# A four-layer gated cross-attention and expert network on one core: context steps ahead, joined projections, and a reordered first stage

## The chip, the core and the metric

The kernel runs on one core of a Trainium2 chip. The metric is device time in microseconds (us). The kernel before was run three times: 908.18 median, 906.4 to 910.17. One more execution was profiled, and all views below come from it.

The engines that matter here: TensorE (PE) multiplies, and its weight loads (PEld) overlap its passes; VectorE (DVE), ScalarE (ACT) and GpSimd (POOL) do the elementwise work; SyncE (SP) issues most DMAs. Each works through its own queue in order.

## The reference

The state x has 16 sequences of 128 tokens with 128 features, and there is a context of the same shape. Eight steps follow each other, each on the layer-normalised x, each gated by a tanh and added:

```python
x = x + tanh(g_xattn[0]) * L0_xattn(ln(x), ctx)   # q + tril(c c^T) q, no softmax
x = x + tanh(g_ffn[0])   * L0_ffn(ln(x))          # 8 experts of 256, top 2
x = x + tanh(g_xattn[1]) * L1_xattn(ln(x), ctx)   # one head, projections in two steps
x = x + tanh(g_ffn[1])   * L1_ffn(ln(x))          # 16 experts of 128, grouped top 4, and shared ones
x = x + tanh(g_xattn[2]) * L2_xattn(ln(x), ctx)   # 16 heads of 8, masked
x = x + tanh(g_ffn[2])   * L2_ffn(ln(x))          # 64 slots, top 8, a gated recurrent update
x = x + tanh(g_xattn[3]) * L3_xattn(ln(x), ctx)   # 16 heads, half of them at half resolution
x = x + tanh(g_ffn[3])   * L3_ffn(ln(x))          # 32 experts of 64, grouped top 8, and shared ones
```

The attention of layer 1 projects twice, with nothing between:

```python
h = lin(x, hW, hb);  c = lin(ctx, cW, cb)
q = lin(h, qW, qb);  k = lin(c, kW, kb);  v = lin(c, vW, vb)
return lin(softmax(q k^T / sqrt(128)) v + q, oW, ob)
```

## The kernel before

**Tiles.** The 16 sequences are four groups of four (GB = 4); the state of a group is X[g], 128 partitions by 512 numbers, and stays in SBUF. CT[g] is the context of a group, transposed, made in the first stage. Everything is in 32-bit floats, and a product of 128x512 shows as two passes.

**The expert layers.** `experts` (L1084) is a stream that walks ORDER: layer 0 for group 0 alone, then layer 1 and layer 3 for four groups each. Each chunk of 128 hidden units is pg and pu (L450, L451), an activation sg on ScalarE (and L456 on VectorE), h = sg * pu on VectorE (L462), hw = h * cb with the routing weights of the chunk on GpSimd (L470) or on VectorE where `on_vector` says so (L468), and two chunks later the product acc (L1092). A chain written out by hand (`in_turn`) keeps the expert products in this order on TensorE. cb is a row of routing weights spread over partitions by a DMA.

**Layer 0 for groups 1 to 3.** Here tokens are sorted by expert. `choose_0` routes them, `places_0` (L904) computes where each goes and issues 24 sends (L940), which are indirect DMAs from GpSimd's queue, a few behind each chunk of group 0 (SEND, and four more at L1161), and the last ones behind the latest rs (L1169). `blocks_0` (L977) reads the sorted rows back as xb (L1006), transposes them (L1013), and works through 31 blocks. `return_0` (L1055) fetches the results during layer 1.

**Who follows whom.** The attention of a group is written into the program when the stream has passed that group: `until(0, g)` pulls the stream until layer 0 is done for group g, then `attention_1(g)` is emitted whole, and so on for `attention_2` and `attention_3` (L1225 to L1229, L1330 to L1339). A scheduler then orders each engine's instructions by when it expects their inputs; `behind_of` pins an instruction behind another on its engine.

**attention_1** (L555) normalises and transposes x, then runs hT, cfT, qT, kT as four products of 128x512 with a biased copy on ScalarE each (L286), v as four products of 128x128, and scores, softmax, output. **attention_2** (L592) and **attention_3** (L729) normalise, transpose, and project queries (qT) and keys (kTm, in two masked copies on VectorE, L296) and values (vp, L480), then loop over sequences. kTm has one buffer, and so has vp.

**The first stage** (`linear_attention`, L509; FIRST, L1187) does layer 0's attention: transpose the context, products of it with itself, the causal mask on VectorE (sm, L522), the normalised x as xn, and the product with sm. `normed` (L246) is the statistics on VectorE (L251, L253), rs by a power on GpSimd (L257), and then either VectorE's subtract and multiply (L268) or, with `on_act`, off on GpSimd (L262, L263) and ScalarE's scale and bias (L266). `blank` (L133) makes zeroed tiles on GpSimd.

Of the kernel before, what the change touches and what calls it, by code (L numbers as in the profile page):

```python
# [59 lines left out]
def flamingo(ctx, tc, x_in, ctx_in, mask_in, w1, w2, w3, wslot, wsmall, slots, cols_in, rows_in, consts_in,  # L60
# [72 lines left out]
    def blank(name, shape):  # L133
        t = const.tile(shape, F32, tag=name, name=name)
        nc.gpsimd.memset(t[:], 0.0)
        return t
# [109 lines left out]
    def normed(g, xn=None, on_act=False):  # L246
# [3 lines left out]
        for t in range(GB):  # L250
            nc.vector.bn_stats(st[:, t, :], x[:, t, :])  # L251
# [8 lines left out]
        if on_act:  # L260
            off = small.tile([P, GB], F32, tag="off", name="off")
            nc.gpsimd.tensor_tensor(off[:], mv[:, :, 0], rs[:], ALU.mult)  # L262
            nc.gpsimd.tensor_scalar(off[:], off[:], -1.0, None, ALU.mult)  # L263
# [245 lines left out]
    def linear_attention(g):  # L509
# [12 lines left out]
        nc.vector.tensor_tensor(sm[:], ps, bc(tri[:], 1, GB), ALU.mult)  # L522
        yield
        xn = normed(g, act.tile([P, GB, D], F32, tag="a1", name="xn0"), on_act=True)
# [29 lines left out]
    w = lambda W, i: W[:, i * D:(i + 1) * D]  # L554
    def attention_1(g):  # L555
        _, xnT = normed_T(g)
        add_row(g, ob1)
        hT = linear_T(w(W1, 0), xnT, "a0", bias=col("hb"))
        cfT = linear_T(w(W1, 1), CT[g], "a1", bias=col("cb"))
        qT = linear_T(w(W1, 2), hT, "qT", bias=col("qb"))  # L560
        kT = linear_T(w(W1, 3), cfT, "kTm", bias=col("kb"), bufs=1)
        pv = split(mm_tile())
        for t in range(GB):
            mm(pv[:, t, :], cfT[:, t * P:(t + 1) * P], w(W1, 4))
        v = act.tile([P, GB, D], F32, tag="a3", name="v1")
        nc.vector.tensor_tensor(v[:], pv, bc(row("vb"), 1, GB), ALU.add)
# [15 lines left out]
        add_gated(g, py, tgx[:, 1:2])  # L582

# [8 lines left out]
    def attention_2(g):  # L592
        _, xnT = normed_T(g)
        add_row(g, ob2)
        qT = act.tile([P, 2, GT], F32, tag="qT", name="qT2")
        kTm = act.tile([P, 2, 2, GT], F32, tag="kTm", name="kTm2", bufs=1)
        for s in range(2):
# [4 lines left out]
            keys_by_head(kTm[:, s], W2H[:, 2 + s, :], CT[g][:], "bk2", s)  # L602
        pv = mm_tile()
        for t in range(GB):
            mm(pv[:, t * P:(t + 1) * P], CT[g][:, t * P:(t + 1) * P], w(W2, 0))
        values(GB, 0, NH, pv[:], bvr)
# [39 lines left out]
        add_gated(g, py, tgx[:, 2:3])  # L646

# [81 lines left out]
    def attention_3(g):  # L729
        _, xnT = normed_T(g)  # L730
        add_row(g, ob3)
        even = CT[g][:, 0:GT:2]
        G2 = GT // 2
        qT = act.tile([P, 3 * G2], F32, tag="qT", name="qT3")
        qa, qb = qT[:, 0:GT], qT[:, GT:]
        kTm = act.tile([P, 2, 3 * G2], F32, tag="kTm", name="kTm3", bufs=1)
        ka, kb = kTm[:, :, 0:GT], kTm[:, :, GT:]
        p = mm_tile()
        mm(p[:], W3H[:, 0, :], xnT[:])
        nc.scalar.activation(qa, p[:], AF.Identity, bias=hcol["bq30"])  # L740
        p = mm_tile()
        mm(p[:, :G2], W3H[:, 1, :], xnT[:, 0:GT:2])
        nc.scalar.activation(qb, p[:, :G2], AF.Identity, bias=hcol["bq31"])
# [8 lines left out]
        values(2, 8, 8, pv[:, 4 * 64:6 * 64], bv3r[:, 4 * 64:])  # L752
        oa = act.tile([P, 2, P], F32, tag="oT", name="oa3")
# [91 lines left out]
        for u in range(2):  # L845
            nc.vector.scalar_tensor_tensor(xv[:, :, u, :], py[u], tgx[:, 3:4], xv[:, :, u, :], ALU.mult, ALU.add)

# [14 lines left out]

    def on_vector(layer, g, n):

        return (layer, g) == (0, BYE - 1) and n > 5 and n % 2 == 0 or (layer, g) == (1, 0) and n < 4
# [218 lines left out]
    def experts():  # L1084
# [23 lines left out]
        for at, (layer, g) in enumerate(ORDER):  # L1108
# [10 lines left out]
            if moving:  # L1119
                for n, k in SEND:  # L1120
                    steps.setdefault(n, []).extend([("m", sending, None)] * k)
                steps.setdefault(13, []).append(("m", "owners", None))
            elif at + 1 < len(ORDER):
# [35 lines left out]
            if moving:  # L1159
                side[0] = "m"  # L1160
                for _ in range(4):  # L1161
# [52 lines left out]

    sending, fetching = places_0(), return_0()
# [8 lines left out]

    until(0, 0)  # L1225
    ob1 = gated_row("ob", tgx[:, 1:2])
    attention_1(0)
    until(0, 1)
# [189 lines left out]
```

## Time and profile before

| what | us |
|---|---|
| median of three runs | 908.18 (906.4 to 910.17) |
| profiled execution, its own time | 908.96 |
| its span, first to last instruction | 907.3 |
| VectorE busy | 571.6 |
| GpSimd busy | 302.0 |
| ScalarE busy | 267.6 |
| one chunk hw on GpSimd / h on VectorE | 1.289 / 0.684 |
| one biased copy of a projection on ScalarE (L286) | 0.687 |
| one masked copy of keys on VectorE (L296, 128x512) | 0.737 |

The stages in the span: first stage and routing to about 34 us; layer 0's experts for group 0 to 90; a stretch to 109; the blocks to 160; layer 1's experts with attention_1 to about 290; attention_2, the slots, attention_3 and layer 3's experts to the end, the last group's experts alone from about 860.

A line of the timeline has start, duration, engine, line, operation, output and inputs, shapes and count, and in brackets how long the engine had stood idle and what ended that. A wait for several things is put down to the one that came last.

### The profile page before, as it was taken

Reading aid. Unit: us, or ns where it says so; the run is one execution under the profiler, and the core shown is the slowest. Engines: PE = TensorE matmul, PEld = TensorE weight load, DVE = VectorE, ACT = ScalarE, POOL = GpSimd, SP = SyncE. Lnnn points to the kernel's source line nnn. Section 1 sums busy time; section 2 is a strip of 40 time slices with the busy share of each in tenths; the row PEclk is TensorE's granted clock in tenths of the full one; section 3 lists DMA queues with packets and bytes.
Section 4 is the critical chain, followed back from the end, with each engine's and each line's share of the span. In section 5 each row is a group of like instructions: output and inputs, shape, how many; then the busy total and the mean of one; then the engine's idle time right before and its main releaser. Section 6 shows DMA issues by size and latency. Waiting matters only on the chain. (4 is left out here: it accounts for less than half of the span.)

```text
span 907.3 us, 16095 instructions
## 1 busy us (share of the span) xinstructions
PE 832.2 (92%) x6191; PEld 465.8 (51%) x6191; DVE 571.6 (63%) x1597; ACT 267.6 (29%) x485; POOL 302.0 (33%) x312
## 2 busy tenths in 40 slices
PE   5898699898999999998999989999999999999997
PEld 4653399344545454554455554555554554555443
DVE  4673344557888657468676667768665668667532
ACT  2522355231322232422322322332222232222321
POOL 4348521556452114113421114321124123313443
PEclk9899799999999999999999999999999999999999
DMA  9441222631221012001212113210002111211230
GB/s 299 134 117 42 61 71 74 220 125 40 85 71 36 13 49 59 24 22 39 71 34 59 38 48 107 80 39 25 25 13 75 46 36 50 81 49 52 92 110 30
DMA packets 55677, 62.12 MB, mean 68 GB/s; under 512 B 14312, under 2 KB 33512, under 8 KB 55472
## 3 DMA queue, kind: packets, MB, share of 16 engines
q1 hardware_dynamic: 53536, 57.67, 20.6%
q0 software_dynamic: 1536, 3.15, 1.2%
q8 instruction: 49, 0.80, 0.4%
q10 hardware_dynamic: 528, 0.26, 0.1%
q14 instruction: 28, 0.23, 0.1%
HBM read 53.97 MB, written 7.09 MB: 67 GB/s over the span
## 5 line engine op out<-in xcount | busy, mean ns | idle before, releaser
L470 POOL TENSOR_TENSOR hw<-h,cb 128x512 f32<-128x512 f32 x137 | 176.6, 1289 | 446.6 <-DVE h L462 371.9
L451 PE MATMUL pu<-xnTx,wall 128*128 128x512 f32 x288 | 153.9, 616 | 7.6 <-DVE sg L456 6.2
L450 PE MATMUL pg<-xnTx,wall 128*128 128x512 f32 x288 | 153.7, 616 | 1.8 <-ACT xnTx L243 1.4
L455 ACT ACTIVATE sg<-pg 128x512 f32<-128x512 f32 x123 | 73.5, 598 | 264.1 <-PE pg L450 251.1
L1092 PE MATMUL acc<-hw,wall 128*128 128x512 f32 x288 | 149.9, 604 | 1.5 <-POOL hw L470 1.5
L462 DVE TENSOR_TENSOR h<-sg,pu 128x512 f32<-128x512 f32 x145 | 99.2, 684 | 62.8 <-PE pu L451 45.5
L456 DVE SCALAR_TENSOR_TENSOR sg<-sg,pg 128x512 f32<-128x512 f32 x123 | 83.5, 679 | 38.9 <-ACT sg L455 38.4
L451 PEld LDWEIGHTS pu<-xnTx,wall 128*128 128x128 f32 x288 | 51.7, 192 | 68.8 <-issue 40.5
L1092 PEld LDWEIGHTS acc<-hw,wall 128*128 128x128 f32 x288 | 53.8, 194 | 61.5 <-issue 53.6
L490 DVE TENSOR_REDUCE mp<-mm 128x4 f32<-128x512 f32 (+1 forms) x112 | 65.8, 645 | 21.1 <-PE mm L617 19.9
L450 PEld LDWEIGHTS pg<-xnTx,wall 128*128 128x128 f32 x288 | 49.8, 193 | 40.8 <-issue 29.0
L504 DVE RECIPROCAL rcw<-po 128x128 f32<-128x128 f32 (+1 forms) x28 | 25.2, 900 | 52.9 <-PE po L499 41.9
L257 POOL TENSOR_TENSOR rs<-ve,neghalf 128x4 f32<-128x4 f32 x32 | 32.8, 1026 | 63.0 <-DVE ve L255 59.4
L496 PE MATMUL po<-pts,vp 128*32 128x128 f32 (+1 forms) x896 | 45.9, 273 | 6.8 <-ACT pts L639 5.9
L639 ACT ACTIVATE pts<-mm 128x512 f32<-128x512 f32 x64 | 33.8, 601 | 55.0 <-PE mm L633 54.6
L268 DVE TENSOR_SCALAR xn<-x,mv,rs 128x128 f32<-128x128 f32 x96 | 35.5, 426 | 21.5 <-POOL rs L257 21.2
L499 PE MATMUL po<-pts,own 128*32 128x128 f32 (+1 forms) x896 | 44.0, 265 | 0.0
L496 PEld LDWEIGHTS po<-pts,vp 128*32 128x32 f32 (+1 forms) x896 | 21.5, 108 | 29.8 <-ACT pts L639 14.6
L241 PE MATMUL tr<-ident,xn 128*128 128x128 f32 x100 | 22.9, 310 | 13.4 <-DVE xn L268 12.2
L251 DVE BATCH_NORM_STATS2 st<-x 128x6 f32<-128x128 f32 x128 | 29.4, 280 | 7.9 <-DMA x<-in_x 7.3
L458 ACT ACTIVATE sg<-pg 128x512 f32<-128x512 f32 x33 | 19.5, 595 | 48.7 <-PE pg L450 46.1
L617 PE MATMUL mm<-kTm,qT 32*128 32x256 f32 x256 | 30.6, 414 | 0.0
(345 smaller groups left out, 1236.1 us busy)
## 6 DMA issues: line engine op xcount, KB each, us to landing
cb<-combD SPq DMA_DIRECT2D x72, 256.0 KB
cb<-combD SPq DMA_DIRECT2D x128, 128.0 KB
wall<-in_gu SPq DMA_DIRECT2D x24, 256.0 KB
wall<-in_dn SPq DMA_DIRECT2D x12, 256.0 KB
xb<-xd SPq DMA_DIRECT2D x7, 256.0 KB
yd<-yb SPq DMA_DIRECT2D x7, 256.0 KB
xd<-vp SPq DMA_DIRECT2D x1, 1072.0 KB
x<-in_x SPq DMA_DIRECT2D x4, 256.0 KB
```

The lines of the kernel that those rows point to most:

```text
L268: nc.vector.tensor_scalar(xn[:, t, :], x[:, t, :], mv[:, t, 0:1], rs[:, t:t + 1], ALU.subtract, ALU.mult)
L450: in_turn(chain, nc.tensor.matmul(out=pg[:], lhsT=w[:, 0], rhs=xnT[:], start=True, stop=True))
L451: in_turn(chain, nc.tensor.matmul(out=pu[:], lhsT=w[:, 1], rhs=xnT[:], start=True, stop=True))
L455: nc.scalar.activation(sg[:], pg[:], AF.Tanh, scale=0.5)
L456: nc.vector.scalar_tensor_tensor(sg[:], sg[:], 1.0, pg[:], ALU.add, ALU.mult)
L462: ins = nc.vector.tensor_tensor(h[:], sg[:], pu[:], ALU.mult)
L470: latest["hw"] = nc.gpsimd.tensor_tensor(hw[:], h[:], cb[:], ALU.mult).ins
L490: nc.vector.tensor_reduce(mp[:, 0:n, 32 * i + 16:32 * i + 18], src, AX.X, ALU.max)
L496: in_turn(chain, nc.tensor.matmul(out=po[32 * jj:32 * jj + 32, 0, :], lhsT=vcols, rhs=pts, start=first, stop=last, skip_group_check=True))
L499: in_turn(chain, nc.tensor.matmul(out=po[32 * jj:32 * jj + 32, 1, :], lhsT=own[rows, r, :], rhs=pts, start=False, stop=last, skip_group_ch ...
L639: nc.scalar.activation(pts[:], split(ps[i]), AF.Exp, scale=scale8)
L1092: in_turn(chain, nc.tensor.matmul(out=acc[0][:], lhsT=w[:, 2], rhs=h[:], start=n == 0, stop=last))
```

## The change

1. *Joined projections.* A new step `joined_1` computes once, from the weights of layer 1, the products of the first and second projection, and the joined biases. `attention_1` then has one product for q, one for k, four small ones for v, and no hT or cfT.
2. *Context steps.* attention_1, 2 and 3 first emit what needs the context alone (k, v; kTm, vp), yield, and emit the rest when the stream has passed (`attend`). The context step of group 0 is emitted in the stream, three chunks after the joining; kT takes buffer a0, no longer kTm.
3. *First stage.* Groups 0 and 1 are normalised by VectorE; of groups 2 and 3 the first statistic is pinned behind the sm of the group before; the memsets of `blank` are pinned behind group 2's off.
4. *Sends.* The last chunk (n = 15) of group 0 multiplies its routing weight on VectorE; two sends, not four, follow the last chunk, so that seven, not five, come behind the latest rs.

```diff
     def blank(name, shape):
         t = const.tile(shape, F32, tag=name, name=name)
-        nc.gpsimd.memset(t[:], 0.0)
+        behind_of("first", nc.gpsimd.memset(t[:], 0.0))
...
-    def normed(g, xn=None, on_act=False):
+    def normed(g, xn=None, on_act=False, behind=None):
...
         for t in range(GB):
-            nc.vector.bn_stats(st[:, t, :], x[:, t, :])
+            ins = nc.vector.bn_stats(st[:, t, :], x[:, t, :])
+            if t == 0 and behind is not None:
+                behind_of(behind, ins)
...
-        xn = normed(g, act.tile([P, GB, D], F32, tag="a1", name="xn0"), on_act=True)
+        xn = normed(g, act.tile([P, GB, D], F32, tag="a1", name="xn0"), on_act=g > 1, behind=("sm", g - 1) if g > 1 else None)
+        if g == 2:
+            latest["first"] = latest["off"]
...
+    def joined_1():
+        pt = tr_tile()
+        for i in range(2):
+            nc.tensor.transpose(pt[:, i * D:(i + 1) * D], w(W1, i), ident[:])
+        firsts = work.tile([P, 4, P], F32, tag="pts", name="firsts", bufs=3)
+        nc.any.tensor_copy(firsts[:, 0:2, :], split(pt)[:, 0:2, :])
+        p = mm_tile()
+        for i, (one, two) in enumerate(((0, 2), (1, 3), (1, 4))):
+            mm(p[:, i * D:(i + 1) * D], firsts[:, one, :], w(W1, two))
+        at = 3 * D
+        mm(p[:, at:at + 1], w(W1, 2), col("hb"))
+        mm(p[:, at + 1:at + 2], w(W1, 3), col("cb"))
+        cbs = work.tile([P, P], F32, tag="rcw", name="cbs")
+        nc.vector.tensor_scalar(cbs[:], ones[:], col("cb"), None, ALU.mult)
+        pb = mm_tile()
+        mm(pb[:, 0:D], cbs[:], w(W1, 4))
+        nc.vector.tensor_copy(W1[:, 0:3 * D], p[:, 0:3 * D])
...
     def attention_1(g):
+        kT = linear_T(w(W1, 1), CT[g], "a0", bias=col("kb"))
+        pv = split(mm_tile())
+        for t in range(GB):
+            mm(pv[:, t, :], CT[g][:, t * P:(t + 1) * P], w(W1, 2))
+        v = act.tile([P, GB, D], F32, tag="a3", name="v1")
+        nc.vector.tensor_tensor(v[:], pv, bc(row("vb"), 1, GB), ALU.add)
+        yield
         _, xnT = normed_T(g)
         add_row(g, ob1)
-        hT = linear_T(w(W1, 0), xnT, "a0", bias=col("hb"))
-        cfT = linear_T(w(W1, 1), CT[g], "a1", bias=col("cb"))
-        qT = linear_T(w(W1, 2), hT, "qT", bias=col("qb"))
-        kT = linear_T(w(W1, 3), cfT, "kTm", bias=col("kb"), bufs=1)
...
+        qT = linear_T(w(W1, 0), xnT, "qT", bias=col("qb"))
...
-        return (layer, g) == (0, BYE - 1) and n > 5 and n % 2 == 0 or (layer, g) == (1, 0) and n < 4
+        return (layer, g) == (0, BYE - 1) and (n > 5 and n % 2 == 0 or n == 15) or (layer, g) == (1, 0) and n < 4
...
+                steps.setdefault(JOIN, []).append(("m", joining, None))
+                steps.setdefault(JOIN + 3, []).append(("m", context_1, None))
...
-                for _ in range(4):
+                for _ in range(2):
                     next(sending)
...
+    def attend(attention, g, *what):
+        steps = attention(g)
+        next(steps)
+        until(*what)
+        next(steps)
...
     for g in range(NG + 1):
         if g < NG:
-            until(1, g)
-            attention_2(g)
+            attend(attention_2, g, 1, g)
         if g > 0:
-            until("slots", g - 1)
-            attention_3(g - 1)
+            attend(attention_3, g - 1, "slots", g - 1)
```

JOIN is 9, a chunk number of group 0. In attention_2 and attention_3 the lines for kTm and vp move unchanged ahead of the first yield.

## Prediction, before the changed kernel was run

> **What bounds the kernel now.** I read part 1 of the page, then the busy times by stage, then the timeline of the stretches where TensorE stands still.
>
> ```profile
> PE 832.2 (92%) x6191; PEld 465.8 (51%) x6191; DVE 571.6 (63%) x1597; ACT 267.6 (29%) x485; POOL 302.0 (33%) x312
> ```
>
> TensorE is busy 832 of 907 us; nothing else comes near. The next view has, for each stretch, its length and then the busy time (and records) of TensorE, its weight loads, VectorE, ScalarE and GpSimd, the granted clock and DMA.
>
> ```profile
> 86.00:109.00 23.00, 13.94 (x43) 6.76 (x41) 6.20 (x19) 3.92 (x6) 15.22 (x16) 0.78 0.20 62
> 109.80:160.00 50.20, 49.48 (x436) 48.90 (x437) 21.46 (x68) 30.15 (x57) 9.15 (x16) 1.00 0.24 68
> 217.00:300.00 83.00, 75.38 (x301) 38.16 (x299) 68.81 (x205) 21.33 (x37) 38.14 (x37) 0.98 0.18 54
> 300.00:860.00 560.00, 528.98 (x4909) 286.93 (x4907) 378.01 (x971) 157.07 (x281) 142.61 (x122) 0.99 0.16 50
> ```
>
> From 109.8 to 160 (the expert blocks of layer 0) and again from 300 to 860 TensorE sets the pace: work taken off it is time. From 217 to 300 VectorE is busy 69 of 83 us too. From 86 to 109 TensorE is not the limit, and the timeline (start, duration, engine, line, in brackets the idle time before and who ended it) tells what is:
>
> ```profile
> 88.82 1.12 PE L1092 MATMUL acc<-hw,wall 128*128 128x512 f32 x2 [1.04 <-POOL hw L470]
> ...
> 95.63 1.05 POOL L257 TENSOR_TENSOR rs<-ve,neghalf 128x4 f32<-128x4 f32 x1
> ...
> 97.20 1.33 PE L241 MATMUL tr<-ident,xn 128*128 128x128 f32 x4 [5.92 <-DVE xn L268]
> ...
> 99.20 2.07 PE L108 MATMUL mm<-xnTm,w 128*128 128x512 f32 x2 [0.68 <-ACT xnTm L243]
> ...
> 103.28 0.96 POOL L940 DMA_INDIRECT xd<-xs,to  x1 [0.30 <-issue]
> ...
> 108.50 0.66 PE L1013 MATMUL tr<-ident,xb 128*128 128x128 f32 x4 [0.74 <-DMA xb<-xd]
> ```
>
> GpSimd issues 24 row sends (one per 1.28 us) between 61.6 and 104.2; the blocks start only when the last has landed and the rows come back, 4.3 us later.
>
> **The change, part by part.** [...]I sum on the span.
>
> *First stage.* Before, the masked products sm of groups 0 and 1 wait on VectorE behind the statistics of group 2, which wait for its DMA at 11.10, and ScalarE's xn waits at 10.72 for GpSimd's off, behind memsets. After, the built order has ScalarE copy both context transposes. But only the first of group 2's four statistics is set behind; the other three still stand ahead of the new xn. So: DMA 11.10, three statistics 0.66, xn of group 0 4 x 0.33 = 13.1, two more xn 0.65, sm 14.4; the eight products of group 0 (1.9) end near 16.9, where the add of x started at 19.30 before. Two xn, sm and the rest follow under that. Layer 0's routing, its comb rows and the first expert chunk come about 2 us earlier (between 0 and 3). The moved memsets (2.4 us) now stand ahead of group 1's second rs, whose result is not due before the transposes of group 0's comb: nothing.
>
> *Expert stage of group 0 (34 to 90).* Added for TensorE: the joining (two transposes 0.22, eight passes of 128x128 0.9, four one-column passes 0.4: 1.5 us), and kT and v of group 0 (0.86 + 0.90 = 1.76), out of the gap. W1 was issued at 53.45 and by the byte rate of that stretch is there near 57; the join's transposes come at 60: no wait. The join falls ahead of a TensorE bubble of 1.1 us (73.2 to 74.3, ScalarE waiting on GpSimd) and costs 0.4 or less; kT and v cost 1.76. VectorE gains 1.7 us of joining where it is busy 58%: nothing. So TensorE arrives at the last chunks where it was (-2 + 2). The last hw goes from GpSimd (ready 88.76) to VectorE (0.69 after h, 87.5): the last acc starts 87.6, not 88.8. The chain acc, yT, transposes, add, ve (4.6 us) ends at 92.2, not 93.45. With two sends fewer ahead, GpSimd is free then: rs at 92.3, not 95.6. Behind it stand three sends, the row add (1.28) and now four sends, not two: the last is issued by 103.8, not 104.24. GpSimd's queue, not the attention, starts the blocks: **-0.5 us**, of 3.3 that rs gains.
>
> *The gap.* xnT, q, scores: two projections fewer and kT, v gone. This shortens 97 to 108 by some 5 us, and all of it goes into the wait for the sends. [...]Row: after 5.92 us idle two passes of 128x512 took 2.07, where the warm pair takes 1.02. [...]Before, TensorE worked from 97 until 107.8 and entered the blocks warm (eight passes in 1.06). [...]I take **+1.7**, since the row at 99.20 shows the half pace after such an idle.
>
> *Blocks.* kT and v of group 1 now lie here, TensorE full: **+1.8**. The blocks end 3.0 later; the fetches behind them, which pace 160 to 187, follow.
>
> *attention_1 of group 1.* Between 190.0 and 199.0 TensorE ran pg, hT, cfT, qT, kT, v, scores and pu, partly at half pace. After: pg 1.3, q 1.7, pu 1.0, scores 0.9, to 194.9: **-4.1**. Of groups 2 and 3 each: context 1.76 earlier (+1.0 where it fills part of a 1.64 us wait at 219, +1.8 for group 3), and hT, cfT, kT, v gone from the attention, 3.5: **-2.5 and -1.7**.
>
> *attention_2 and attention_3.* No work goes; 3.6 us of VectorE (four kTm of 0.74, vp 0.68) and about 3 of TensorE stand ahead of the wait for the expert group, not after it. TensorE's waits that this queue makes are mp's: 1.64 at 296.75, 0.74 at the start of each of four attention_3. At most 1.6 + 4 x 0.74 = 4.6 goes. Where attention_2 follows attention_3 directly nothing moves but the order. The added wait: kTm has one buffer, so its write waits for the last scores of the attention before, and h, sg and the next statistics stand behind it on VectorE. Below, -4.6; above, four to seven times an uncovered 3.6. After attention_2 of group 0 a dozen TensorE passes of 0.86 stand before the next xn transposes, so it is mostly covered: **-2**.
>
> Sum: -0.5 + 1.7 + 1.8 - 4.1 - 2.5 - 1.7 - 2.0 = **-7.3**: span 900.0, and on the median of runs 908.2 - 7.3 = 900.9.
>
> **Rivals.**
> (a) *As summed*, 900.9. For it: full TensorE on both sides, 5.2 us of passes gone for good (six linears of 0.86). Chance 0.52.
> (b) *The saving turns into waits.* From 217 to 300 VectorE has 69 of 83 us, loses nothing, and each attention's softmax is its work; if groups 2 and 3 give nothing (-4.2 lost) and mp's waits only move (-2 lost): 908.2 - 1.1 = 907. The first stage's 2 us not coming would cost 1.5 more. Against it: TensorE still worked 75 of those 83 us. Chance 0.24.
> (c) *Slower:* the context operations block VectorE at the head of its queue, at the seven transitions from one attention to the next; each holds h back by up to 3.6 us, and TensorE's in-order queue with it. It decides from 1.0 us uncovered per transition (7.3 / 7), and at 2.0 gives 900.9 + 14 = 915. For it: kTm's single buffer, VectorE 67% busy from 300 to 860. Against: the passes that lie between. Chance 0.11.
> (d) *More:* all of mp's 4.6 goes, no cold start (-1.7), and attention chains that are 3 us shorter take 2 more off later waits: 900.9 - 2.6 - 1.7 - 2 = 894.6. Chance 0.13.
> That a part doesn't do what it says is in the first stage: three of four statistics are not set behind. It takes 1 to 2 us there, most of which the sends would have swallowed.
>
> **How the numbers follow.** Likeliest 900.9. Case (a) alone spans 897 to 905: the bounds of the first stage, the cold start and the waits, 2 us each. The range reaches over (d) nearly and into (b): 894.5 to 909; outside lie (c) and the rim of (d). A measurement of this kernel tells about 0.5% (4.5 us) from no change: faster is below 903.6. From (a) most (0.46 of 0.52), (d) all, (b) 0.05: 0.64. Same: the rest of (a), most of (b), a little of (c): 0.25. Slower: 0.11.
>
> **What would show it.** First stage: the first add of x near 17, the first expert matmul near 31.5. rs behind the last add near 92, the last send issued near 104, transposes of xb near 108, the first block passes at twice 1.06 per eight. The blocks end near 163; scores of group 1 near 196 to 198; the last expert stage, 47 us long, starts about 7 earlier and is as long as before. I am wrong if the sends end later than 104.5, if new waits of TensorE on kTm, vp or h show at the transitions, or if the xb wait shrinks by more than 1 us.

## The result and the profile after

Ten runs of each kernel on one chip: the changed kernel 913.75 us median (907.71 to 915.30), the kernel before 908.5 (906.40 to 913.12). The ratio is 1.0045, with a 95% interval of 1.0025 to 1.0065: about 4 us slower (5 by the medians), where 7.3 less were predicted. The profiled execution took 915.29 us, span 913.6; before it was 908.96 and 907.3.

Part 1 of the page of the changed kernel (busy time, share of the span, instructions):

```profile
PE 831.8 (91%) x6189; PEld 466.9 (51%) x6189; DVE 578.4 (63%) x1610; ACT 260.7 (29%) x470; POOL 299.1 (33%) x307
```

This is the first thing to see. Eight products of 128x512 are gone (hT and cfT of four groups, 0.86 each, 6.9 us) and the joining brought 1.5, so TensorE should be busy 5.4 us less. It is busy 831.8 us, where it was 832.2, and it stands idle 81.7 us, where it was 75.0. The clock is a part of this: 46.5 us of its busy time lie in windows at half clock, where it was 31.0. These are the sums of the view of stretches over all half-clock windows, of the changed kernel and then of the kernel before:

```profile
sum 58.90, PE 46.48 PEld 27.58 DVE 26.70 ACT 12.21 POOL 18.32; mean PE 5.17 PEld 3.06 DVE 2.97 ACT 1.36 POOL 2.04
sum 34.12, PE 30.94 PEld 15.45 DVE 17.37 ACT 9.56 POOL 17.33; mean PE 4.42 PEld 2.21 DVE 2.48 ACT 1.37 POOL 2.48
```

The view of stretches (length, then busy time and records of TensorE, its weight loads, VectorE, ScalarE, GpSimd, then the granted clock) shows where, in the same two windows as in the prediction:

```profile
217.00:300.00 83.00, 71.42 (x257) 35.15 (x255) 68.48 (x204) 17.74 (x32) 37.49 (x37) 0.95 0.17 54
300.00:860.00 560.00, 525.80 (x4927) 285.08 (x4927) 378.00 (x970) 155.06 (x278) 140.38 (x121) 0.99 0.15 48
```

From 217 to 300 TensorE is busy 4 us less and idle so much more, and the granted clock fell from 0.98 to 0.95.

The stretch before the blocks went as predicted. The timeline of the changed kernel (lines of GpSimd and TensorE picked out):

```profile
93.03 1.04 POOL L259 TENSOR_TENSOR rs<-ve,neghalf 128x4 f32<-128x4 f32 x1 [0.77 <-DVE ve L257]
...
103.20 0.96 POOL L977 DMA_INDIRECT xd<-xs,to  x1 [0.30 <-issue]
...
108.32 1.12 PE L1050 MATMUL tr<-ident,xb 128*128 128x128 f32 x4 [6.78 <-DMA xb<-xd]
```

rs came 2.6 us earlier than before (95.63), the last send only 0.08 (103.28), the transposes of xb 0.18 (108.50). TensorE's idle time before them grew from 0.74 to 6.78 us, and the four transposes took 1.12 us where they had taken 0.66. This is one execution of each. In the six traces whose program up to here is the changed kernel's (three of them with dead products in the wait), xb comes between 105.4 and 108.3, and in the three with the old first stage between 108.5 and 108.9.

To see where the time was lost, I compare the start of the same product h on VectorE in both traces. They come in the same order, 172 of them, and are counted here from 0.

| h | what lies there | before | after | shift |
|---|---|---|---|---|
| 0 | first expert chunk | 36.34 | 34.34 | -2.0 |
| 15 | last chunk of group 0 | 86.30 | 86.83 | +0.5 |
| 31 | last block | 158.33 | 161.03 | +2.7 |
| 40 | before attention_1 of group 1 | 190.49 | 194.77 | +4.3 |
| 44 | after it | 208.38 | 208.22 | -0.2 |
| 48 | before the routing weights come to TensorE | 232.61 | 230.90 | -1.7 |
| 52 | after attention_1 of group 2 | 248.35 | 252.85 | +4.5 |
| 58 | after attention_1 of group 3 | 274.91 | 275.51 | +0.6 |
| 85 | third group of layer 1 done | 444.62 | 450.19 | +5.6 |
| 120 | first group of layer 3 done | 690.80 | 702.81 | +12.0 |
| 154 | third group of layer 3 done | 854.84 | 861.16 | +6.3 |

A shift in the middle of the table is partly order alone: a context step that is made one stage earlier delays the chunks of that stage and relieves the next. What is left at the end is not.

The largest single step is between h 48 and h 52. TensorE alone, in the timeline of the changed kernel:

```profile
232.02 1.02 PE L108 MATMUL mm<-xnTm,w 128*128 128x512 f32 x2
...
233.82 1.16 PE L108 MATMUL mm<-a,qT 128*128 128x128 f32 x8 [0.78 <-ACT qT L288]
238.42 1.02 PE L423 MATMUL tr<-ident,comb 128*16 128x128 f32 x4 [3.44 <-DVE comb L380]
239.23 1.91 PE L452 MATMUL pg<-xnTx,ws 128*128 128x512 f32 x2
240.94 1.92 PE L453 MATMUL pu<-xnTx,ws 128*128 128x512 f32 x2
242.64 1.55 PE L1129 MATMUL acc<-hw,wall 128*128 128x512 f32 x2
```

and the same place in the kernel before:

```profile
233.72 1.02 PE L108 MATMUL mm<-xnTm,w 128*128 128x512 f32 x2
234.58 1.02 PE L108 MATMUL mm<-cT,w 128*128 128x512 f32 x2
235.52 1.99 PE L108 MATMUL mm<-a,w 128*128 128x512 f32 x4
237.34 1.05 PE L108 MATMUL mm<-w,a 128*128 128x128 f32 x8
238.28 1.16 PE L108 MATMUL mm<-kTm,qT 128*128 128x128 f32 x8
239.28 0.60 PE L421 MATMUL tr<-ident,comb 128*16 128x128 f32 x4
239.71 1.02 PE L450 MATMUL pg<-xnTx,ws 128*128 128x512 f32 x2
```

Behind the scores TensorE's next instruction is the transposes of comb, layer 1's routing weights for group 1. VectorE makes comb in a chain of some twenty small operations that nothing of the change shortens. (It even takes longer: the row maxima of the scores, 0.68 us, now stand ahead of comb in VectorE's queue, and comb starts 0.68 us after the operation before it in its chain, not 0.21.) Before, the four projections filled the time until comb was there. After, they are gone, and TensorE stands still for 3.44 us. Then comes a second charge: the transposes (1.02 us, not 0.60) and three pairs of passes (1.91, 1.92 and 1.55 us, not 1.02) run slower, 2.3 us on the pairs alone. Three stretches of 3.4 us of this trace (same columns as above) show the granted clock there:

```profile
233.46:236.88 3.42, 1.16 (x8) 0.97 (x8) 3.34 (x17) 0.31 (x1) 2.54 (x3) 1.00 0.06 19
236.88:240.29 3.41, 1.87 (x6) 1.13 (x7) 1.98 (x7) 0.81 (x2) 2.38 (x4) 0.50 0.13 38
240.29:243.71 3.42, 3.42 (x6) 1.35 (x5) 2.28 (x5) 0.89 (x2) 0.00 (x0) 0.50 0.27 80
```

TensorE was busy 1.16 us of the first stretch, at a granted clock of 1.00. In the second it was busy 1.87 us and in the third 3.42, both at 0.50; from 243.71 on the clock is 1.00 again. Between 115 and 890 us the changed kernel spends 30.7 us at half clock, the kernel before 17.1.

How much is the wait, and how much the clock? At half clock pg and pu start 1.71 us apart here (239.23 and 240.94), at full clock 0.86 (239.71 and 240.57). So as an estimate, half of TensorE's busy time at half clock is what the clock cost. The shift then splits into three parts (us):

| stretch | shift | TensorE idle | half of its busy time at half clock | the rest of its busy time |
|---|---|---|---|---|
| h 44 to h 58 | +0.8 | +3.1 | +0.9 | -3.3 |
| h 58 to the end | +5.7 | +4.0 | +5.1 | -3.4 |
| whole span | +6.3 | +6.7 | +7.8 | -8.2 |

So what the change saved in work (8.2) nearly came back as waits (6.7), and the clock made a loss of it. Of the 3.4 behind h 58, 2.9 are score products of attention_2 that the profile shows with shorter times; why was not followed.

### The profile page after: what moved, and what is told of

Its sections match the earlier page's. It is cut to its first block, busy times and chain, and to the rows that moved or that the text cites. A ratio compares the mean times of both kernels' runs of the same rounds, so it can differ in the third digit from the quotient of the medians.

```text
span 913.6 us, 16066 instructions
## 1 busy us (share of the span) xinstructions
PE 831.8 (91%) x6189; PEld 466.9 (51%) x6189; DVE 578.4 (63%) x1610; ACT 260.7 (29%) x470; POOL 299.1 (33%) x307
## 4 chain that ended last, share of the span: by engine, by line
PE 35%; DVE 15%; issue 7%; POOL 6%; ACT 2%; DMA 2%; SPq 0%; POOLq 0%; ACTq 0%; DVEq 0%
PE mm L108 6%; PE acc L1129 5%; POOL hw L472 5%; PE pg L452 5%; PE pu L453 4%; PE po L498 2%; DVE mp L492 2%; DVE h L464 2%; PE mm L649 2%; DVE sg L458 2%; PE mm L665 2%; PE po L501 2%; DVE xn L270 1%; PE mm L644 1%; DVE rcw L506 1%
## 5 line engine op out<-in xcount | busy, mean ns | idle before, releaser
L472 POOL TENSOR_TENSOR hw<-h,cb 128x512 f32<-128x512 f32 x136 | 174.2, 1282 | 454.7 <-DVE h L464 338.2
L1129 PE MATMUL acc<-hw,wall 128*128 128x512 f32 x288 | 152.8, 614 | 0.5 <-POOL hw L472 0.5
L458 DVE SCALAR_TENSOR_TENSOR sg<-sg,pg 128x512 f32<-128x512 f32 x123 | 83.4, 678 | 52.9 <-ACT sg L457 52.7
L270 DVE TENSOR_SCALAR xn<-x,mv,rs 128x128 f32<-128x128 f32 x104 | 38.2, 420 | 19.8 <-POOL rs L259 19.8
L259 POOL TENSOR_TENSOR rs<-ve,neghalf 128x4 f32<-128x4 f32 x32 | 32.7, 1023 | 48.4 <-DVE ve L257 46.5
L498 PEld LDWEIGHTS po<-pts,vp 128*32 128x32 f32 (+1 forms) x896 | 22.1, 108 | 30.7 <-ACT pts L671 17.4
L251 DVE BATCH_NORM_STATS2 st<-x 128x6 f32<-128x128 f32 x128 | 31.5, 302 | 8.0 <-DMA x<-in_x 7.5
L649 PE MATMUL mm<-kTm,qT 32*128 32x256 f32 x256 | 30.7, 423 | 0.0
```

What stands on the lines that cost most here:

```text
L458: nc.vector.scalar_tensor_tensor(sg[:], sg[:], 1.0, pg[:], ALU.add, ALU.mult)
L472: latest["hw"] = nc.gpsimd.tensor_tensor(hw[:], h[:], cb[:], ALU.mult).ins
L498: in_turn(chain, nc.tensor.matmul(out=po[32 * jj:32 * jj + 32, 0, :], lhsT=vcols, rhs=pts, start=first, stop=last, skip_group_check=True))
L649: nc.tensor.matmul(out=split(ps[i])[:, 2 * s:2 * s + 2, :], lhsT=qT[rr, s, b], rhs=kTm[rr, s, :, b], start=False, stop=True, skip_group_ch ...
L1129: in_turn(chain, nc.tensor.matmul(out=acc[0][:], lhsT=w[:, 2], rhs=h[:], start=n == 0, stop=last))
```

## Theories and experiments

**Theory A, cover:** what was taken out or made ahead had filled TensorE's waits for VectorE. Without it the waits show, and in or behind some of them the clock is halved: here at the 3.44 us above (TensorE busy 1.16 us of 3.42, then a granted clock of 0.50) and at a wait of 2.53 us at 297.10 (busy 1.22 us of 3.42, then 0.50). The "under about half busy" of the first expectation is my estimate from such stretches of this trace. **Theory B** is my rival (c): keys and values ahead hold up VectorE's queue at the transitions from one attention to the next.

All ratios are to the kernel before, run beside it on the same chip (its median was 908.2 to 908.5, and 909.9 for the control and for both fills). The microseconds are the ratio's distance from 1 times 908.3; the medians can tell another 1 to 2 us, most of all for kernels with six runs (context steps of attention_2 and 3, 3 dead products in group 2, 3 and 5).

| kernel | median | ratio (95%) | us |
|---|---|---|---|
| the change | 913.75 | 1.0045 (1.0025 to 1.0065) | +4.1 |
| first stage alone | 906.1 | 0.9975 (0.9963 to 0.9988) | -2.3 |
| joined projections alone | 907.0 | 0.9986 (0.9974 to 0.9998) | -1.3 |
| context steps of attention_2 and 3 alone | 914.03 | 1.0068 (1.0048 to 1.0088) | +6.2 |
| the change without context steps | 904.2 | 0.9959 (0.9945 to 0.9974) | -3.7 |
| that, with attention_1's | 908.25 | 0.9992 (0.9974 to 1.0010) | -0.7 |
| that, with attention_3's | 907.52 | 0.9987 (0.9975 to 1.0000) | -1.2 |
| that, with attention_2's | 910.33 | 1.0025 (1.0009 to 1.0041) | +2.3 |
| the change, dead products in attention_1 | 909.98 | 0.9995 (0.9974 to 1.0016) | -0.5 |
| the change, 4 dead products before the blocks | 913.5 | 1.0053 (1.0036 to 1.0071) | +4.8 |
| the change, 6 dead products before the blocks | 909.41 | 1.0009 (0.9993 to 1.0025) | +0.8 |
| the change, both fills (4 and 6) | 906.34 | 0.9966 (0.9943 to 0.9989) | -3.1 |
| no context steps, 3 dead products in group 2 | 902.86 | 0.9927 (0.9900 to 0.9954) | -6.6 |
| no context steps, the same in group 3 (control) | 906.31 | 0.9969 (0.9950 to 0.9987) | -2.8 |
| no context steps, 3 and 5 dead products | 900.17 | 0.9889 (0.9864 to 0.9915) | -10.1 |

### Each part alone

The first stage (item 3) put into the kernel before:

```diff
-        xn = normed(g, act.tile([P, GB, D], F32, tag="a1", name="xn0"), on_act=True)
+        xn = normed(g, act.tile([P, GB, D], F32, tag="a1", name="xn0"), on_act=g > 1, behind=("sm", g - 1) if g > 1 else None)
...
-        nc.gpsimd.memset(t[:], 0.0)
+        behind_of("first", nc.gpsimd.memset(t[:], 0.0))
```

> The kernel before with the reordered first stage alone (nothing else of the change). Theory A (cover: what was taken out or moved ahead had filled TensorE's waits for VectorE, and a wait that leaves TensorE under about half busy in one 3.4 us stretch halves its clock in the next): the first expert chunk starts about 2 us earlier, near 31.6; the sends from GpSimd's queue start earlier by as much, so that part of it survives to the blocks; total 906.5 to 909, no loss. Theory B (context operations block VectorE at the transitions between attentions): the same, since no context operation is touched. If this alone is slower by 3 us or more, both are wrong about where the loss lies.

Measured: -2.3 us, 906.1, just below the 906.5 to 909. The transposes of xb came at 104.99, 3.5 us earlier than in the kernel before, so the sends did not swallow the gain.

The joined projections put into the kernel before, with k and v where they were:

```diff
+                steps.setdefault(JOIN, []).append(("m", joining, None))
...
-        hT = linear_T(w(W1, 0), xnT, "a0", bias=col("hb"))
-        cfT = linear_T(w(W1, 1), CT[g], "a1", bias=col("cb"))
-        qT = linear_T(w(W1, 2), hT, "qT", bias=col("qb"))
-        kT = linear_T(w(W1, 3), cfT, "kTm", bias=col("kb"), bufs=1)
+        qT = linear_T(w(W1, 0), xnT, "qT", bias=col("qb"))
+        kT = linear_T(w(W1, 1), CT[g], "a0", bias=col("kb"))
```

> The kernel before with the joined projections alone: the joining stands in the stream of group 0 as in the change, attention_1 keeps its place and makes k and v after the normalised x, with no context step. Theory A: four passes of 128x512 (1.7 us) and two biased copies go from each attention_1; at the attention_1 of group 2 TensorE then waits 1.0 to 2.5 us for the routing weights of layer 1 (k and v still cover 1.7 us of the 3.4 that the whole change opens), and of 5 to 7 us of work 0 to 3 survive: 905 to 909. Theory B: work is removed and no context operation moves, so all of it survives: 901 to 904.

Measured: -1.3 us, in A's range and outside B's. The wait for comb is there, 2.11 us at 238.74.

The context steps of attention_2 and 3 put into the kernel before:

```diff
-            until(1, g)
-            attention_2(g)
+            attend(attention_2, g, 1, g)
...
-            until("slots", g - 1)
-            attention_3(g - 1)
+            attend(attention_3, g - 1, "slots", g - 1)
```

> The kernel before with the context steps of attention_2 and attention_3 alone (keys and values ahead of the wait for the expert group), nothing else. Theory A: TensorE's waits for the first row maxima of attention_2 grow from 1.6 and 0 to about 2.5 and 1.7 us, some of them halve the clock of the next stretch, and attention_3's starts gain about 0.5 each: 908 to 914, slower by 0 to 6. Theory B: keys written ahead hold VectorE's queue up at the seven transitions: 915 or more, with waits of TensorE for kTm, vp or h of over 1 us at each of them.

Measured: +6.2 us. A expected up to 6, B 7 or more, so the time does not tell them apart. The trace does, in part. TensorE's waits for the row maxima mp are as A has them; two of them in this kernel's timeline:

```profile
296.78 0.47 PE L626 MATMUL tr<-ident,mp 128*128 128x128 f32 x1 [2.53 <-DVE mp L490]
...
504.39 0.44 PE L626 MATMUL tr<-ident,mp 128*128 128x128 f32 x2 [1.69 <-DVE mp L490]
```

The first was 1.64 before, and at the second no wait is shown. No wait of TensorE for kTm, vp or h over 1 us appears, which B asked for. And VectorE does not stand still for the keys. The view of the tile kTm, writes by VectorE, says how long it sat idle ahead of them (us, times), first in the kernel before, then in the changed one (2.2 in this kernel too):

```profile
  PE mm L108: 8.6, 4
```

```profile
  PE mm L108: 2.2, 7
```

The four idle times of 2.15 us before attention_3's keys are gone. So B falls as it was put: keys and values do not wait. But VectorE's queue is held up at another place, and this is where the longer waits for mp come from. The scores, the next normalised x and the row maxima, first in the kernel before, then in the kernel of this run:

```profile
496.85 1.13 PE L617 MATMUL mm<-kTm,qT 32*128 32x256 f32 x12
497.23 1.12 DVE L268 TENSOR_SCALAR xn<-x,mv,rs 128x128 f32<-128x128 f32 x4 [1.13 <-POOL rs L257]
498.26 2.48 DVE L490 TENSOR_REDUCE mp<-mm 128x4 f32<-128x512 f32 x4
```

```profile
498.42 1.14 PE L620 MATMUL mm<-kTm,qT 32*128 32x256 f32 x14
499.06 1.26 POOL L470 TENSOR_TENSOR hw<-h,cb 128x512 f32<-128x512 f32 x1 [13.28 <-issue]
501.34 0.60 DVE L268 TENSOR_SCALAR xn<-x,mv,rs 128x128 f32<-128x128 f32 x2 [2.33 <-POOL rs L257]
501.85 2.48 DVE L490 TENSOR_REDUCE mp<-mm 128x4 f32<-128x512 f32 x4
```

The row maxima stand behind xn in VectorE's queue, and xn waits for rs from GpSimd, which is busy with hw until 500.32. Before, VectorE wrote keys and values between the statistics and xn; now they are written ahead of the statistics, and xn waits 2.33 us, not 1.13. The scores are done at 499.56 and mp starts at 501.85, 2.3 us later, where it was 0.3.

The change without any context step (every attention makes keys and values after `until`, as before):

```diff
-    context_1 = attention_1(0)
     until(0, 0)
-    next(context_1)
-    attend(attention_1, 1, 0, 1)
+    attention_1(0)
+    until(0, 1)
+    attention_1(1)
```

> The changed kernel without any context step: first stage, joined projections and the earlier sends stay, and every attention makes its keys and values after the wait for the expert group, as before. Theory A: the cover is back in attention_2 and attention_3, and k and v cover part of attention_1's wait: 904 to 909, that is 5 to 9 below the changed kernel. Theory B: the context steps are the whole loss: 900 to 903. If it stays near 913, neither the cover nor the context steps are the cause.

Measured: -3.7 us, 904.2, at the low edge of A's range. So the first stage, the joining and the sends are worth their keep (-2.3 and -1.3 alone make -3.6; the sends had no run of their own), and the context steps cost 7.8 us (1.0045 less 0.9959).

### The context steps one by one

Attention_1's, put back alone on that kernel:

```diff
     for g in range(2, NG):
-        until(0, g)
-        attention_1(g)
+        attend(attention_1, g, 0, g)
```

> The changed kernel with the context step of attention_1 only; attention_2 and attention_3 make keys and values after the wait for the expert group, as before. The kernel with no context step at all came to 904.2, the whole change to 913.75. Theory A (cover): the step of attention_1 takes k and v (1.76 us) out of the stretch before the wait for layer 1's routing weights, where the wait then grows from 2.58 to about 3.4 us, and puts them into the blocks, where TensorE is full: 906.5 to 909; the larger part of the loss lies in attention_2 and attention_3. Theory B (VectorE's queue held up at the transitions): 904 to 906.

Measured: 3.0 us more than without (0.9992 less 0.9959; 4.0 by the medians). The wait for comb is 3.44 us at 237.01, where it was 2.58.

Attention_3's:

```diff
-            until("slots", g - 1)
-            attention_3(g - 1)
+            attend(attention_3, g - 1, "slots", g - 1)
```

> The kernel without context steps (904.2) with the context step of attention_3 alone put back. Theory A: attention_3 started with a wait of 0.74 us for its first row maxima four times, and keys made ahead let its scores start earlier; its keys and values cost the same work earlier, where the tail of the attention before leaves TensorE waits: 901.5 to 904.5, no loss. The loss of the context steps then lies in attention_2. Theory B: each of the four transitions into attention_3 holds VectorE's queue up: 906 or more.

Measured: 2.5 us more, 907.5 (3.3 by the medians). A's number was wrong: I had counted the four waits of 0.74 that go (they did go) and not those that open elsewhere. In this trace the waits that are new or longer are 1.28 for comb at 427.89, 1.19 and 1.20 for the slots' products (0.53 before), and 2.31 for the last group's xn at 827.75. TensorE's idle time grew by 2.8 us in sum. The keys did not lie under these waits: the last are written by 743, 85 us ahead of that xn. What the trace shows there is another order: a chunk's sg and h stand ahead of xn on VectorE (from 824.54), where without the step they come behind it. That this follows from the cover was not shown. B's number (906 or more) fits, but VectorE's idle time before keys and values is 1.7 us here and 8.9 without the step.

Attention_2's:

```diff
-            until(1, g)
-            attention_2(g)
+            attend(attention_2, g, 1, g)
```

> The kernel without context steps (904.2) with the context step of attention_2 alone put back. The steps of attention_1 and attention_3 alone cost 4.0 and 3.3 us on that kernel. Theory A (cover): if the three are independent, attention_2's is the rest of 913.75 - 904.2, 2.2 us: 905.5 to 908, with waits for the first row maxima of 2.5 and 1.7 us where it had 1.64 and none. If it is 904 or less, two of the steps only lose together; if 909 or more, they cover for each other. Theory B (VectorE's queue held up by keys and values) is out by the traces, in which VectorE's idle time ahead of these operations fell from 8.9 to 2.2 us.

Measured: 6.0 us more, 910.3, outside the 905.5 to 908 that independence gave. The waits are those expected (2.53, 1.69 and 1.69 us). The three steps cost 3.0, 2.5 and 6.0 alone, 11.5 in sum, and 7.8 together. With an interval of 1 to 2 us on each number, the difference is no more than the noise: whether they are independent is open.

The profiles say what the steps of attention_2 and attention_3 change in the end. From h 58 to the end of the span, a stretch of about 630 us, with TensorE's busy time summed over the half-clock windows in it:

| kernel | length | TensorE busy at half clock | length less half of that |
|---|---|---|---|
| before | 632.3 | 6.8 | 628.9 |
| no context steps | 629.5 | 0.0 | 629.5 |
| no context steps, control | 634.3 | 10.2 | 629.1 |
| the change | 638.1 | 17.0 | 629.6 |
| the change, both fills | 632.2 | 6.7 | 628.9 |

In all sixteen traces the last column lies between 628.5 and 631.7, with the context steps and without. So in these traces what the steps cost lies in the clock: the six traces that have both spend 14.1 us of TensorE's work at half clock in the mean, the eight with neither 6.0. The change and both fills have the same order of work on VectorE, ScalarE and GpSimd in this stretch, and differ by 5.9 us. No run filled the waits of attention_2 or attention_3, so this is read from the traces and not tested.

### Is it the wait, or the clock that follows it?

Dead products decide this: work for TensorE whose result nothing uses. In the changed kernel, four of them between q and the scores of group 2, written to the bank that the scores overwrite:

```diff
+        ps = mm_tile()
+        fill = filled(ps[:], 4, latest["linear"]) if g in (2,) else []
+        ps = split(ps)
...
+            if fill:
+                in_turn(fill, scored)
```

where `filled` issues n products of the identity with CT[0] in a chain.

> The changed kernel with four dead products of 128x512 (3.4 us of TensorE) put between q and the scores of group 2's attention_1, where hT, cfT, kT and v were before; their result is overwritten by the scores and used by nothing. In the changed kernel TensorE waits 3.44 us there for the routing weights, and then runs two 3.4 us stretches at half clock, in which three pairs of passes take 1.9, 1.9 and 1.55 us instead of 1.0 each. Theory A with the clock as amplifier: the wait is filled, the clock stays full, about 2.3 us are gained: 910.5 to 912.5, and the next transposes of comb start within 0.3 us of where they were. If only the wait counts and not the clock: 913.5 to 914. If the work on TensorE counts, 916 or more.

Measured: 909.98, 4.5 us less than the change by the ratios (3.8 by the medians), more than the 1.3 to 3.3 expected. TensorE in the timeline of this kernel:

```profile
231.51 3.60 PE L450 MATMUL mm<-cT,ident 128*128 128x512 f32 x8
...
236.59 0.61 PE L423 MATMUL tr<-ident,comb 128*16 128x128 f32 x4 [0.59 <-DVE comb L380]
237.03 1.02 PE L458 MATMUL pg<-xnTx,ws 128*128 128x512 f32 x2
```

From q to the transposes of comb it is 5.94 us, where the changed kernel has 6.40 (the scores come later, and comb no longer stands behind their row maxima), and the three pairs of passes that follow take 1.02 us each (1.91, 1.92 and 1.55 in the changed kernel). The order of a few chunk passes behind this place moved as well, so I repeated it where nothing else moves: three dead products in the kernel without context steps.

> The kernel without context steps (904.2) with three dead products of 128x512 between q and the scores of group 2's attention_1; every other instruction keeps its place on every engine. There TensorE waits 2.58 us for the routing weights, and then runs 3.4 us at half clock. With the clock as amplifier: 1 to 2 us are gained, 902 to 903.5. If only the wait counts: 904.2. If the dead work counts: 906 or more.

Measured: 902.9; by the ratios 2.9 us less than without them (0.9959 less 0.9927), by the medians 1.3, with intervals that overlap; on VectorE, ScalarE and GpSimd the two traces have the same order throughout. The pair of timelines, first without dead products, then with:

```profile
232.82 1.16 PE L108 MATMUL mm<-a,qT 128*128 128x128 f32 x8
236.56 0.80 PE L423 MATMUL tr<-ident,comb 128*16 128x128 f32 x4 [2.58 <-DVE comb L380]
237.15 1.92 PE L452 MATMUL pg<-xnTx,ws 128*128 128x512 f32 x2
```

```profile
230.65 2.74 PE L450 MATMUL mm<-cT,ident 128*128 128x512 f32 x6
233.23 1.05 PE L605 MATMUL mm<-a,qT 128*128 128x128 f32 x8
234.12 0.60 PE L423 MATMUL tr<-ident,comb 128*16 128x128 f32 x4
234.56 1.02 PE L458 MATMUL pg<-xnTx,ws 128*128 128x512 f32 x2
```

Useless work of 2.6 us costs nothing here, and the first pair of passes behind comb takes 1.02 us, not 1.92. The control puts the same three where TensorE does not wait, in attention_1 of group 3:

```diff
-        fill = filled(ps[:], 3, latest["linear"]) if g in (2,) else []
+        fill = filled(ps[:], 3, latest["linear"]) if g in (3,) else []
```

> The kernel without context steps (904.2) with three dead products of 128x512 between q and the scores of attention_1, but of group 3, not of group 2; every other instruction keeps its place. At this place TensorE goes from product to product without a wait. If dead products help only where they fill a wait and keep the clock: 2.6 us (three times 0.86) are lost, less the 0.95 us that TensorE waits for aT 12 us later at most: 905.5 to 907. If dead products help for another reason (their place in the program, the banks): 902.5 to 904, as in group 2.

Measured: 906.3, in the range of the loss. By the ratios it is 3.8 us above the kernel with the same products in group 2, but only 0.9 above the kernel without any, with intervals that overlap. The trace is clearer: from h 49 to h 67 this kernel takes 111.3 us, 2.9 more than without dead products (108.4), and the kernel with them in group 2 takes 107.5. The first two have one half-clock window in this stretch, behind the wait for comb; the last has none.

### The cold start of the blocks

Dead products behind the scores of group 0 in the changed kernel, four and then six:

```diff
+        if g == 0:
+            filled(mm_tile()[:], 4, scored.ins)
```

> The changed kernel with four dead products of 128x512 behind the scores of group 0's attention_1, in the 6.8 us in which TensorE stands idle before the blocks; their result is used by nothing. At half clock they take 6.9 us, and so they end with the wait for the sent rows. With the clock as amplifier: the first stretch of the blocks runs at full clock, the first product h of the blocks comes 1.5 to 2 us earlier against the transposes of xb than in the changed kernel, and all that follows with it: 911.5 to 912.5. If the cold start costs nothing: 913.5 to 914.5. If the dead work delays the blocks: 914.5 or more.

Measured: 913.5, no gain, but the question stayed open: the four ended 2.57 us before the rows were back and did not fill the wait. So six:

> The changed kernel with six dead products of 128x512, not four, in the idle time of TensorE before the blocks (four ended 2.6 us before the sent rows were back, and the clock still fell). If six last until the rows are back, the blocks start at full clock: from the transposes of xb to the end of the blocks 50.9 to 51.7 us where the changed kernel takes 52.7, and 911.5 to 913 in all. If the cold start is worth nothing: 52.5 or more, and 913.5 or more.

Measured: 909.4, 3.3 us less than the change by the ratios and more than expected. TensorE waited 0.74 us for xb, and from the transposes of xb (105.44) to the last h of the blocks (155.97) it took 50.5 us, where the changed kernel took 52.7 (108.32 to 161.03). The cold start was worth 2.2 us. (The order of some block instructions moved with the dead products. That xb itself came 2.9 us earlier is not their doing: in this execution the first chunk had already started 2.1 us earlier.)

Both fills in the changed kernel:

> The changed kernel (913.75) with both fills: four dead products in attention_1 of group 2 (alone 3.8 less) and six before the blocks (alone 4.3 less). If the two waits with their clock are separate parts of the loss, they add: 905 to 907.5, and 1 to 3 us of the distance to the kernel without context steps (904.2) remain, for attention_2 and attention_3. If the two gains were one shift of the clock's grid, 909 to 910.

Measured: 906.3, by the ratios 7.2 us below the change; one by one they gave 4.5 and 3.3. They are separate parts of the loss. And the version that the experiments point to, the change without context steps, with three dead products in group 2 and five before the blocks:

> As the kernel before this one (no context steps, three dead products in group 2's attention_1), with five more dead products in the 5.4 us in which TensorE stands idle before the blocks; the order of some block instructions shifts with them. With the clock as amplifier at both places: 900.5 to 903. If the dead products outlast the wait for the sent rows at half clock, the blocks start up to 1 us later: 903 to 905.

Measured: 900.2, just below the 900.5 to 903, ratio 0.9889 (0.9864 to 0.9915): faster than both kernels, by 1.1% (0.9% by the medians) and about 1.5%, with eight products that compute nothing.

## Why the prediction was wrong, step by step

*First stage: right alone, mis-sized as a part.* The first chunk came 2.0 us earlier. I had the sends swallow nearly all of it; alone it carried through to the end, -2.3. (The first chunk starts between 31.6 and 34.9 in the thirteen traces with the new stage, and between 35.8 and 36.6 in the three with the old.) In the change the joining and the context step of group 0 use it up again: the last h of that stage is 0.5 late.

*Sends and gap: right,* though of the -0.5 the pair of traces has 0.2. Last send at 103.20 (by 103.8), xb at 108.32 (near 108), rs at 93.0 (92.3).

*Cold start, +1.7: right in sign, somewhat larger.* No run shows the term as I summed it; what the runs showed in its place is 2.2 us (52.7 for the blocks in the changed kernel, 50.5 with six dead products ahead of them). In the trace of the changed kernel the granted clock is 0.50 from 93.52 to 114.00, 5.7 us into the blocks; in that of the kernel before it is back at 1.00 at 105.12, ahead of them. I weighed the clock here, and only here: at every other new wait it stood in my sum at nothing.

*kT and v of group 1 in the blocks, +1.8: too much.* With a warm start on both sides the blocks took 50.5 us with them (six dead products) and 49.8 in the kernel before, +0.7: TensorE was not full there, it had 1.3 us of waits in the blocks, and 0.35 are left. (Against the best kernel, 48.7, it is +1.9, but there the order of the blocks had moved.) The blocks ended 2.7 later and I had 3.0; that this is so near is luck, since 0.2, 2.2 and 0.7 stand for my 0.5, 1.7 and 1.8.

*"attention_1 of group 1: -4.1": right.* From h 40 to h 44 the shift went from +4.3 to -0.2. Some 1.7 of it is a half-clock window of the kernel before (190.45 to 193.86) that the changed kernel does not have there. (Just ahead, between h 31 and h 40, both kernels have a wait, 3.63 us before and 3.83 after; TensorE was busy 3.42 us at half clock behind it before, from 173.38 to 176.80, and 6.17 us after, from 175.44 to 182.27: +1.4 by the estimate above.)

*"Of groups 2 and 3: -2.5 and -1.7": this step failed.* From h 44 to h 58 the shift went from -0.2 to +0.6: nothing was gained where 4.2 was summed. I priced the four projections at their own duration, because TensorE was busy 75 of 83 us around them. But the instruction behind them waited for a chain on VectorE that they had covered. In group 2 the 3.5 us taken out came back as a wait of 3.44 for comb and two windows at half clock (236.88 to 243.71). Over both groups 3.3 us of work went, TensorE's idle time grew by 3.1, and the clock cost 0.9 more than it had before. My rival (b) had named this turn of a saving into a wait, but priced it at zero and not below it.

*"attention_2 and attention_3: -2": this step failed, with the sign.* From h 58 to the end the shift grew from +0.6 to +6.3, and these context steps alone cost 6.2 us. The waits of 0.74 that I wanted gone did go. But "mostly covered" was said of the wrong side: I asked what hides the moved work, and not what the moved work hides. On VectorE keys and values had stood between the statistics and the row maxima; without them there the three waits for maxima of attention_2 are 2.53, 1.69 and 1.69, and with those for comb and xn TensorE's idle time grew by 4.0 us. The term that made it a loss is one that I had put at nothing: five windows at half clock, two of them behind waits for maxima and three behind waits for oT (1.74 us, before 1.56), where the kernel before has two. By the estimate above that is 5.1 us more.

*Rival (c), slower by a blocked VectorE:* the sign and nearly the time were its (915), the mechanism in the main was not: VectorE's idle time before the keys fell to a quarter, and no wait of TensorE for kTm, vp or h over 1 us came. One part of it did come true in attention_2, that the next statistics stand behind the keys on VectorE; what then waited was mp. None of the three signs of being wrong that the prediction named appeared.

## What to carry to other kernels

Before taking work off an engine that is busy 90% of the time, look at the next instruction in its queue: if that waits for a chain on another engine, the work was cover, and its removal is worth only what that wait does not take back. Work that needs no late input is the best cover there is; making it "as early as possible" spends it where nothing has to be covered. Where saved work and new waits nearly balanced, as behind h 58 here, the clock decided. So price a new wait on TensorE twice, once for itself and once for the half clock that may follow it (in the traces of the two kernels it came with eleven of the sixteen waits of 1.56 to 3.83 us listed below); dead products in the wait are a fair test of that, and here even a gain.

## What the runs showed of the hardware

At some waits of TensorE the granted clock fell to 0.50, at others it stayed at 1.00. Between 115 and 890 us the trace of the kernel before has five stretches at 0.50, of 3.41 us each (17.1 in sum), that of the changed kernel six, three of 3.41 and three of 6.83 us (30.7). Each begins in one of TensorE's waits of 1.56 us and more, or less than 2 us behind it (us, with the start of the instruction that waited):

| trace | fell to 0.50 | stayed at 1.00 |
|---|---|---|
| before | 3.63 (173.18), 1.91 (189.07), 1.64 (219.40), 1.56 (656.95), 2.12 (759.74) | 1.64 (296.75), 1.56 (533.10) |
| after | 3.83 (176.09), 3.44 (238.42), 2.53 (297.10), 1.69 (505.01), 1.74 (537.29), 1.74 (665.57) | 1.92 (193.35), 1.69 (633.79), 2.32 (834.54) |

So in these two traces the length of the wait alone does not tell which it is. In one execution of the kernel before, the same wait for oT comes twice with 1.56 us, at 533.10 and at 656.95. In the 3.41 us from 531.79 TensorE was busy 2.10 us, and the clock stayed at 1.00; in the 3.41 us from 654.67 it was busy 1.85 us, and the stretch behind them ran at 0.50:

```profile
531.79:535.20 3.41, 2.10 (x15) 1.27 (x16) 2.23 (x5) 0.00 (x0) 0.00 (x0) 1.00 0.02 5
535.20:538.60 3.40, 3.14 (x29) 1.37 (x32) 2.43 (x5) 0.00 (x0) 1.25 (x1) 1.00 0.00 0
```

```profile
654.67:658.08 3.41, 1.85 (x18) 1.09 (x17) 2.20 (x6) 0.00 (x0) 0.00 (x0) 1.00 0.00 1
658.08:661.50 3.42, 3.42 (x8) 1.41 (x5) 3.13 (x5) 0.00 (x0) 0.01 (x1) 0.50 0.00 0
```

The time of one kernel's runs went with the granted clock. The change with dead products in attention_1 ran from 902.6 us, with a granted clock of 0.978 over the span, to 911.4 with 0.967; over its 14 runs time and clock have a correlation of -0.87. The ten runs of the change have a clock of 0.968 in the mean, 58 of the kernel before 0.979. Single profiles can be off by several us: the profiled span without context steps is 12.1 us below that of the change, and the medians differ by 9.6. Whether such waits make the spread was not tested.
